# Expert rows: from a scatter into two rows per token to an accumulating scatter into one, with the surplus branch moved behind the last store

## The chip, the cores and the metric

The kernel runs on one core of one Trainium2 chip. The metric is the device time of one execution in microseconds (us). The core has five engines with a queue each: TensorE (PE, matrix products), VectorE (DVE), ScalarE (ACT), GpSimd (POOL) and SyncE (SP, which here only issues DMAs). Data moves between DRAM and the on-chip memory SBUF by DMA; an indirect DMA takes its row numbers from a table and is issued from POOL.

## The reference

The input x has 16 batches of 256 tokens with 256 values, 4096 tokens in all. Each batch has a profile number that selects an adapter, and the layer-normed output of the adapter goes through a shared two-layer network and through the two best of eight experts:

```python
z = relu(x @ Wd[profile] + bd[profile])
y = x + z @ Wu[profile] + bu[profile]
h = (y - mean(y)) * rsqrt(var(y) + 1e-5) * g[profile] + b[profile]

p = softmax(h @ gate_w + gate_b)                 # 8 experts
value, index = top_k(p, 2)
value = value / (sum(value) + 1e-9)
mlp(h, w1, b1, w2, b2) = gelu(h @ w1 + b1) @ w2 + b2     # 256 -> 1024 -> 256
moe = sum over the 2 experts of value[e] * mlp(h, ew1[e], eb1[e], ew2[e], eb2[e])
out = x + h + mlp(h, sh_w1, sh_b1, sh_w2, sh_b2) + moe
```

## The kernel before

**Numbers.** Every float32 operand of a large product is split into two float16 halves, and three of the four half products are summed. So a product `mm1` or `mm2` is a group of six matmuls.

**Order.** Nearly all instructions are entered with `plan.op(engine, duration, function, v, deps, acq, rel, after=...)`. `Plan.schedule` works out a start for each from the given durations and due times `v`, and this gives the order in which each engine's queue is written. The real waits are set by the compiler's semaphores from what each instruction reads and writes. An engine works through its queue in order.

**Stages.** `base` (SBUF, 32 tiles of 128 tokens by 256 values) holds the sum that becomes the output.

1. Adapter, layer norm, gate and routing, batch by batch. `payload` makes the split activation rows. `route` finds the two experts of each token and its slot, POOL writes the token's row numbers behind the payload (L1100), and an indirect DMA scatters the rows to their slots in DRAM, `xslot` (L1111). `table` counts slots, pads them and works out which blocks exist. Beside this, PE runs the shared network on batches 0 to 12 (`shared`), whose result is added to `base` (L1355).
2. Experts. There are 37 units: 16 static ones (two blocks of 256 tokens for each expert, weights prepared by `Prep`), 16 dynamic ones of 256 tokens, and 5 of 128 tokens, whose weights are loaded again from `scr` (`block_weights`). `block_T` loads a unit's rows transposed and its row numbers `idt`. `plan_unit` runs the first product, the activation and the split (`hh`), `plan_g2` the second product. On each of the 69 result tiles of 128 tokens, DVE scales it and adds the bias (`take`, L1261, into one of four buffers `ysb`; the profile calls that space `late`), and POOL scatters it with an indirect DMA to `yrow` in DRAM, which has two rows for each token (`scatter_y`, L1267). `apart` declares that these scatters never touch the same rows, so none waits for another.
3. During the dynamic units, ACT's queue reloads x (L1555) and POOL adds x and the shared bias to `base` (L1562, L1563). For the first six batches (`EARLY`), SP loads the rows of `yrow` written by the static units (L1523), DVE adds them with their routing weight `wts` (`sum_one`, L1534), and SP stores the batch (L1539). The weights come from `top2_weights`.
4. After the last expert unit and the first product of shared batch 13, all engines reach a branch (L1631). It is taken only where more blocks exist than the static program covers, or where an early batch has rows beyond the static units; for these inputs it is jumped over.
5. Behind it: the rest of batch 13, batches 14 and 15, the loads of `yrow` for batches 6 to 15 (five of 1 MB), the weighted sums (L1689 on ACT, L1696 on DVE, L1704 on POOL), ten stores.

Of the kernel before, what the change touches and what calls it, by code (L numbers as in the profile page):

```python
# [19 lines left out]
P = 128  # L20
# [15 lines left out]
TOP_AT = 18  # L36
EARLY = 6
# [7 lines left out]
PW = 544  # L45
NBUF = 3
# [98 lines left out]


P_V = (82.0, 121.0)
PACE = (0.0, 9.6, 24.7, 16.4)
VE2 = 8.9

TV, WV, PU2, VP = 22.0, 21.0, 10.32, 8.0
# [3 lines left out]
def adapter_moe_kernel(  # L155
# [25 lines left out]
    yrow = dp.tile([2 * NT, D], F32, tag="yrow", name="yrow")  # L181
# [50 lines left out]
    idb = [const([P, 2, 2], F16, f"idt{i}") for i in range(8)]  # L232
    idx_half = const([P, 2, 2], F16, "idh")
# [45 lines left out]
    plan.pool("id", 8)  # L279
    plan.pool("ysb", 4)  # L280
# [23 lines left out]
    def constants():  # L304
# [50 lines left out]
        )  # L355

    metaf = const([1, 2, NFULL], I32, "metaf")
    metah = const([1, NHALF], I32, "metah")
    used = const([P, 2], I32, "used")
# [355 lines left out]
    def plan_unit(  # L715
# [8 lines left out]
        for c in range(NC):  # L724
# [20 lines left out]
            if c % 4 == 3:  # L745
                def hi(act, q=q, hb=hb):
                    split_hi(hhb[plan.slot["hh", k]], h32b[plan.slot["h32", hb]], tail, q, n, act)

                def lo(q=q, hb=hb):
                    split_lo(hhb[plan.slot["hh", k]], h32b[plan.slot["h32", hb]], tail, q, n)  # L750

                h = plan.op(
                    ("DVE", "ACT") if free_hi else "ACT",
                    ((0.87, 1.1) if full else (0.5, 0.65)) if free_hi else 1.1,
                    (lambda hi=hi: hi(False), lambda hi=hi: hi(True))
                    if free_hi else (lambda hi=hi: hi(True)), vc + 1.0,
                    [ge[-1]], acq=[("hh", k)] if q == 0 else (), lat=0.05,
                )
                quads.append(
                    plan.op(  # L760
                        "DVE", 1.28 if full else 0.7, lo, vc + 2.0, [h], rel=[("h32", hb)], lat=0.05
                    )
                )
# [262 lines left out]
    def route(g):  # L1026
# [68 lines left out]
        for b in (2 * g, 2 * g + 1):  # L1095
            prev = []
            for c in range(2):
                it = plan.op(
                    "POOL", 0.2,
                    lambda b=b, c=c: POOL.iota(  # L1100
                        payb[plan.slot["pay", b]][:, :, 2 * D : PW].bitcast(I32),
                        pattern=[[2 * P, 2], [0, (PW - 2 * D) // 2]],
                        base=4 * P * b + c, channel_multiplier=2,
# [32 lines left out]
    def table(last):  # L1136
        def rt(shape, dt, name):
# [3 lines left out]
        pc2 = lambda: pt_of("count")[:, E : 2 * E]  # L1141
        cnt = plan.op(
            "PE", 0.2,
            lambda: (
                PE.matmul(pc(), ones, mc[:, NG, :], start=True, stop=True),
                PE.matmul(pc2(), ones, mc[:, EARLY // 2, :], start=True, stop=True),
            ), 0.0,
# [10 lines left out]
        over = rt([P, 1], F32, "over")  # L1158
# [5 lines left out]
        for e in range(E):  # L1164
# [12 lines left out]
            lambda: V.tensor_reduce(over, pc2(), AX.X, ALU.max),  # L1177
# [47 lines left out]
        def meta():  # L1225
# [11 lines left out]
            V.tensor_scalar(over, over, float(NSTAT * BLK), 64.0, ALU.is_gt, ALU.mult)  # L1237
            V.tensor_copy(used[:, 0:1], ends[:, 1, E - 1 : E])
            V.tensor_scalar(used[:, 1:2], over, ends[:, 1, E - 1 : E], None, ALU.add)
# [9 lines left out]
    def block_T(u, xgT, idt):  # L1249
        for t in range(u["nt"]):  # L1250
# [7 lines left out]
            SP.dma_start(idt[:, t, :], src[:, 2 * D : 2 * D + 2])  # L1258
# [5 lines left out]

    def scatter_y(ysb, idt, t):
        POOL.memset(spot, 0.0)
        ins = POOL.indirect_dma_start(  # L1267
            out=yrow[:, :],
            out_offset=bass.IndirectOffsetOnAxis(ap=idt[:, t, :].bitcast(I32), axis=0),
            in_=ysb,  # L1270
            in_offset=None,
            bounds_check=2 * NT - 1,
            oob_is_err=False,
        )
        apart("ysc", ins)
# [74 lines left out]
    def shared(b, v, only1=False):  # L1350
        def evac(t, mm, v, rel):
            dst = base[:, 2 * b + t, :]
            plan.op(
                "DVE", 0.45,
# [3 lines left out]
            )  # L1358
# [3 lines left out]
            [tc_done[b]], pE.done, [pE.tail1], free_hi=only1, only1=only1,  # L1362
            behind=g1_last[NU - 1] if only1 else None,
        )

    for b in range(NSH):
        shared(b, U0 + b * PU)
# [7 lines left out]
    plan.op(  # L1375
        "SP", 0.45, lambda: SP.dma_start(sb2_b, sb2.partition_broadcast(P)), 150.0, land=P * 1024
    )
    prep = {}
# [13 lines left out]
    sc_last, W, g1_of, vu_of = {}, {}, {}, {}  # L1392

    def expert_unit(s, vu):
# [27 lines left out]

        def evac(t, mm, v, rel):
            if nt == 1:
                rel = (*rel, ("wf", ("half", s)))
            ty = plan.op(
                "DVE", 0.45,
                lambda: take(ysbb[plan.slot["ysb", (s, t)]], py_of(t, ("e", s)), u["tail"]),
                v, [mm, *ev_deps], acq=[("ysb", (s, t))], rel=rel,
            )  # L1430

            def sc():
                scatter_y(ysbb[plan.slot["ysb", (s, t)]], idb[plan.slot["id", s]], t)

            sc_last[s] = plan.op(
                "POOL", 1.36, sc, v + 0.5, [ty], after=[sc_last.get(s, sc_last.get(s - 1))],
                rel=[("ysb", (s, t))] + ([("id", s)] if t == nt - 1 else []), land=P * 1024,
# [7 lines left out]
        g1_last[s], g1_of[s], vu_of[s] = g1[-1], g1, vu  # L1445
# [6 lines left out]
    for e in range(E):  # L1452
        if e >= 2:
# [3 lines left out]
            else:  # L1457
# [3 lines left out]
                after = [ev_last[NSTAT * (e - 3)] if e > 3 else pads[-1]]  # L1461
            prep[e] = Prep(e, v_of(NSTAT * (e - 1)) - VP, after=after, split_after=split)
# [4 lines left out]


    wts = const([P, 2, NTILE], F32, "wts")
    wlate = const([P, 2, 2 * EARLY], F32, "wlate")  # L1470

    def top2_weights(v):
        T8 = [P, NTILE, E]
        rs, den = const([P, NTILE], F32, "rs"), const([P, NTILE], F32, "den")
        rk, beyond = const([P, 2, 2 * EARLY], I32, "rk"), const([P, 2, 2 * EARLY], F32, "beyond")
        tmp, ex = [z.rearrange("p (j e) -> p j e", e=E) for z in ztb]
        o = plan.op(
            "DVE", 0.4,
            lambda: V.tensor_tensor(tmp, L, m1.unsqueeze(2).broadcast_to(T8), ALU.subtract),
            v, [*gate_of.values(), sli_of[NG - 1], *ydone.values(), ev_last[12]],  # L1480
        )
        o = plan.op("ACT", 3.0, lambda: ACT.activation(ex, tmp, AF.Exp), v, [o])
        fns = [lambda: V.tensor_reduce(rs, ex, AX.X, ALU.add), lambda: V.reciprocal(rs, rs)]
        for c in range(2):
            fns += [
                lambda c=c: V.tensor_tensor(tmp, ex, oh[:, c], ALU.mult),
                lambda c=c: V.tensor_reduce(wts[:, c, :], tmp, AX.X, ALU.add),
                lambda c=c: V.tensor_tensor(wts[:, c, :], wts[:, c, :], rs, ALU.mult),
            ]
        e2 = slice(0, 2 * EARLY)  # L1490
        fns += [
            lambda: V.tensor_tensor(den, wts[:, 0, :], wts[:, 1, :], ALU.add),
            lambda: V.tensor_scalar(den, den, 1e-9, None, ALU.add),
            lambda: V.reciprocal(den, den),
            lambda: V.tensor_tensor(
                wts, wts, den.unsqueeze(1).broadcast_to([P, 2, NTILE]), ALU.mult
            ),
            lambda: V.tensor_scalar(rk, sli[:, :, e2], EBLK * P - 1, None, ALU.bitwise_and),
            lambda: V.tensor_scalar(beyond, rk, float(NSTAT * BLK), None, ALU.is_ge),
            lambda: V.tensor_tensor(wlate, wts[:, :, e2], beyond, ALU.mult),  # L1500
            lambda: V.tensor_tensor(wts[:, :, e2], wts[:, :, e2], wlate, ALU.subtract),
        ]
        return tiny(fns, v, [o], dur=0.22, first=0.4)

    wts_op = top2_weights(0.0)
    for b in range(EARLY):
        plan.op(
            "SP", 0.5,
            lambda b=b: SP.dma_start(
                yrow[2 * b * S : 2 * (b + 1) * S, :].rearrange("(p k) d -> p k d", p=P),  # L1510
                padrow[:, 0 : 2 * D].bitcast(F32).unsqueeze(1).broadcast_to([P, 4, D]),
            ), 60.0 + 12 * b, after=[ln_done[2 * b + 4]], land=99,
        )
# [7 lines left out]

    def y_load(yl, t0, nt):
        SP.dma_start(  # L1523
            yl.rearrange("p j c d -> p j (c d)"),
            yrow[2 * P * t0 : 2 * P * (t0 + nt), :].rearrange("(j p c) d -> p j (c d)", p=P, c=2),
        )
        return yl

    def y_view(flat, nt):
        return flat.bitcast(F32).rearrange("p (j c d) -> p j c d", c=2, d=D)[:, 0:nt]  # L1530

    def sum_one(b, yl, t, c, w):
        j = 2 * b + t
        V.scalar_tensor_tensor(  # L1534
            base[:, j, :], yl[:, t, c, :], w[:, c, j : j + 1], base[:, j, :], ALU.mult, ALU.add
        )

    def store(b):
        SP.dma_start(  # L1539
# [5 lines left out]
    early_buf = [y_view(flat[:, o * 1024 : (o + 2) * 1024], 2) for o in (4, 6)]  # L1545
    plan.pool("xr", 2)
    plan.pool("ey", 2)
    wf_free = [prep[E - 1].tail, *prep[E - 1].done]
    for b in range(NB):
        s = TOP_AT + 1 + b  # L1550
        xr = xlnT[:, 2 + b % 2].rearrange("p l k s -> p (l k s)").bitcast(F32)
        xr = xr.rearrange("p (t d) -> p t d", t=2)
        o = plan.op(
            "ACT", 0.45,
            lambda b=b, xr=xr: ACT.dma_start(  # L1555
                xr, x[b * S : (b + 1) * S, :].rearrange("(t p) d -> p t d", p=P)
# [219 lines left out]
```

## Time and profile before

| | |
|---|---|
| median of 3 runs | 642.57 us (641.12 to 643.31) |
| profiled execution | 643.85 us |
| its span, first to last instruction | 642.1 us |
| PE / DVE / ACT / POOL busy | 605.6 / 405.8 / 404.3 / 234.2 us |
| expert scatters | 69, first issued at 233.8 us, last at 601.7 us |
| PE, last matmul before the branch ends | 600.9 us |
| PE, first matmul behind the branch | 604.26 us |
| last matmul / last store issued | 638.3 / 638.9 us |
| DRAM read / written | 96.46 MB / 44.42 MB |

"Busy" is the time in which an engine executes. The landing of a DMA is the time from its issue until its data is in place and its semaphore is set; for an indirect DMA the busy time on POOL is only the making of its descriptors. The DMA share is the mean busy share of the sixteen DMA engines.

### The profile page before, as it was taken

How to read it: one execution, taken by the hardware profiler on the slowest of the kernel's cores; microseconds unless marked ns; L12 is line 12 of the kernel's file. 1: busy time of each engine (PE TensorE's matmuls, PEld its weight loads, DVE VectorE, ACT ScalarE, POOL GpSimd, SP SyncE). 2: the span in 40 equal slices, each digit the busy share in tenths (PEclk: the TensorE clock that was granted, in tenths of full speed). 3: DMA queues.
4: the chain of work that ended last, by engine and by line, in shares of the span. 5: the costliest groups of instructions: out<-in, count | busy, mean ns of one | idle time of the engine just before them, and what ended most of it. 6: DMA issues, size and time to landing. Idle time of an engine off the chain costs nothing. (4 is left out here: it accounts for less than half of the span.)

```text
span 642.1 us, 15142 instructions
## 1 busy us (share of the span) xinstructions
PE 605.6 (94%) x5542; PEld 522.8 (81%) x5542; DVE 405.8 (63%) x969; ACT 404.3 (63%) x632; POOL 234.2 (36%) x370
## 2 busy tenths in 40 slices
PE   5599999999999999999999999999988998999795
PEld 3368887888988888888888888998967977888684
DVE  5688889899873643775586664455446545545287
ACT  1378576796876867988878755554554535555372
POOL 1003566185387012222221321252325483643143
PEclk7779999999999999999999999999999999999798
DMA  7885558847422276789975698559967699770292
GB/s 262 274 271 168 181 190 309 311 165 264 139 93 105 51 233 140 269 191 273 305 225 154 201 297 267 149 150 300 325 158 257 166 331 258 248 179 19 66 350 98
DMA packets 95783, 134.70 MB, mean 210 GB/s; under 512 B 53691, under 2 KB 73173, under 8 KB 87766
## 3 DMA queue, kind: packets, MB, share of 16 engines
q1 hardware_dynamic: 83778, 108.89, 56.6%
q0 software_dynamic: 6768, 18.43, 8.1%
q10 hardware_dynamic: 5156, 6.35, 3.3%
q8 instruction: 45, 0.74, 0.5%
q14 instruction: 36, 0.29, 0.2%
HBM read 96.46 MB, written 44.42 MB: 219 GB/s over the span
## 5 line engine op out<-in xcount | busy, mean ns | idle before, releaser
L704 PEld LDWEIGHTS <-hh 128*128 128x128 f16 x2424 | 235.1, 98 | 38.4 <-DVE hh L689 9.8
L675 ACT ACTIVATE h<-bank,tst 128x256 f32<-128x256 f32 x256 | 136.0, 560 | 127.8 <-PE bank L668 86.8
L704 PE MATMUL bank<-wst,hh 128*128 128x256 f16 x1536 | 205.8, 273 | 3.3 <-DVE hh L689 3.3
L668 PE MATMUL bank<-late,wst 128*128 128x256 f16 x1536 | 200.4, 273 | 5.0 <-ACT h L675 4.3
L1267 POOL DMA_INDIRECT yrow<-late,idt x69 | 77.6, 1125 | 256.7 <-DVE late L1261 202.6
L668 PEld LDWEIGHTS <-wst 128*128 128x128 f16 x1536 | 150.1, 98 | 23.3 <-issue 4.8
L668 PE MATMUL bank<-xlnT,wsh 128*128 128x256 f16 x768 | 106.6, 279 | 3.4 <-ACTq L1631 3.4
L704 PE MATMUL bank<-wsh,hh 128*128 128x256 f16 x768 | 104.7, 277 | 3.4 <-DVE hh L689 3.4
L675 ACT ACTIVATE h<-bank,tsh 128x256 f32<-128x256 f32 x128 | 70.1, 560 | 58.7 <-PE bank L668 55.1
L689 DVE SCALAR_TENSOR_TENSOR hh<-h,tst,hh 128x1024 f16<-128x1024 f32 x64 | 89.4, 1396 | 27.5 <-ACT hh L683 26.0
L668 PEld LDWEIGHTS <-wsh 128*128 128x128 f16 x768 | 75.5, 100 | 15.5 <-issue 3.8
L1111 POOL DMA_INDIRECT xslot<-late,sli x64 | 70.4, 1101 | 38.5 <-issue 22.4
L1261 DVE SCALAR_TENSOR_TENSOR late<-bank,tst 128x256 f32<-128x256 f32 x64 | 30.5, 483 | 65.0 <-PE bank L704 64.8
L685 DVE TENSOR_SCALAR hh<-h,tst 128x1024 f16<-128x1024 f32 x27 | 21.3, 787 | 46.3 <-ACT h L675 46.3
L689 DVE SCALAR_TENSOR_TENSOR hh<-h,tsh,hh 128x1024 f16<-128x1024 f32 x32 | 42.0, 1311 | 13.4 <-ACT hh L683 13.1
L683 ACT ACTIVATE hh<-h,tst 128x1024 f16<-128x1024 f32 x37 | 42.5, 1148 | 1.1
L683 ACT ACTIVATE hh<-h,tsh 128x1024 f16<-128x1024 f32 x29 | 33.3, 1147 | 0.8
L1100 POOL IOTA late<- 128x32 int32 x32 | 4.8, 161 | 73.4 <-PE bank L977 37.8
L623 DVE SCALAR_TENSOR_TENSOR wst<-wf,prep,wst 128x1024 f16<-128x1024 f32 x20 | 25.3, 1279 | 0.7 <-ACT wst L617 0.7
L842 PE MATMUL bank<-xlnT,wst 128*128 128x256 f32 x64 | 20.6, 453 | 4.7 <-DMA wst<-in_adp_dram 4.7
L1563 POOL TENSOR_TENSOR base<-base,sb_b 128x512 f32<-128x512 f32 x16 | 24.2, 1515 | 1.3
L1562 POOL TENSOR_TENSOR base<-base,xlnT 128x512 f32<-128x512 f32 x16 | 20.6, 1285 | 8.2 <-DMA xlnT<-in_x_dram 8.0
(234 smaller groups left out, 582.2 us busy)
## 6 DMA issues: line engine op xcount, KB each, us to landing
wst<-scr SPq DMA_DIRECT2D x32, 1024.0 KB
scr<-wst SPq DMA_DIRECT2D x16, 1024.0 KB
wf<-scr SPq DMA_DIRECT2D x10, 1024.0 KB
wf<-in_ew_dram SPq DMA_DIRECT2D x5, 1028.0 KB
wf<-in_ew_dram SPq DMA_DIRECT2D x5, 1024.0 KB
wst<-in_adp_dram SPq DMA_DIRECT2D x16, 256.5 KB
xlnT<-in_xT_dram SPq DMA_DIRECT2D x16, 256.0 KB
base<-in_x_dram SPq DMA_DIRECT2D x16, 256.0 KB
```

Source lines behind the costliest of these rows:

```text
L623: V.scalar_tensor_tensor(self.w[:, a + 2048 : b + 2048], self.wf[h][:, f], sc[:, 2 * h : 2 * h + 1], self.w[:, a:b], ALU.mult, ALU.subtract,)
L668: mm = PE.matmul(pa[:, 0:n_tok], w1[:, wl, c, k, :], xin[:, xl, k, 0:n_tok], start=i == 0, stop=i == len(seq) - 1,)
L675: ACT.activation(h32[:, c % 4, 0:n_tok], pa[:, 0:n_tok], AF.Gelu_apprx_tanh, bias=tail[:, c : c + 1], scale=tail[:, 8:9],)
L683: ACT.activation(hi, h4, AF.Copy, scale=tail[:, 9:10])
L685: V.tensor_scalar(hi, h4, tail[:, 9:10], None, ALU.mult)
L689: V.scalar_tensor_tensor(hh[:, 1, c, 0:n_tok], h32[:, :, 0:n_tok], tail[:, 9:10], hh[:, 0, c, 0:n_tok], ALU.mult, ALU.subtract,)
L704: PE.matmul(py, hh[:, hl, k, t * P : (t + 1) * P], w2[:, wl, k, :], start=q == 0 and i == 0, stop=q == 3 and i == len(seq) - 1,)
L842: PE.matmul(pt_of(("z", b))[:, 0:S], wa()[:, k * P : (k + 1) * P], xf32(b)[:, k, :], start=k == 0, stop=k == KC - 1,)
L1111: ins = POOL.indirect_dma_start(out=xslot[:, :], out_offset=bass.IndirectOffsetOnAxis(ap=sli[:, c, j : j + 1], axis=0), in_=payb[plan.slot ...
L1261: V.scalar_tensor_tensor(ysb, py, tail[:, 10:11], tail[:, 11 : 11 + D], ALU.mult, ALU.add)
L1267: ins = POOL.indirect_dma_start(out=yrow[:, :], out_offset=bass.IndirectOffsetOnAxis(ap=idt[:, t, :].bitcast(I32), axis=0), in_=ysb, in_of ...
L1563: POOL.tensor_tensor(bb, bb, sb2_b.unsqueeze(1).broadcast_to([P, 2, D]), ALU.add)
```

## The change

- `yrow` (two rows a token) becomes `yacc` (one row a token, 128 more for padding). Four DMAs from DRAM to DRAM fill it with x (`y_init`) during the first stage. The reload of x and its addition on POOL go.
- Each payload row carries two numbers: where its routing weight lies in a table `wtab` in DRAM, and its token's row.
- `top2_weights` runs before the experts and is written to `wtab`. For each result tile POOL fetches 128 weights with an indirect DMA (`row_weights`), and DVE multiplies the tile by them.
- The scatter adds to the rows of `yacc` (`compute_op=ALU.add`). It is no longer declared free of overlap with the other scatters.
- All of the loads of the sums (now 16 of 256 KB), the additions and the stores come after the last scatter. The early sums and stores go.
- The branch stands behind the last store, and the two plans become one. Some due times and modelled durations are set anew.

```diff
-P_V = (82.0, 121.0)
-PACE = (0.0, 9.6, 24.7, 16.4)
-VE2 = 8.9
-TV, WV, PU2, VP = 22.0, 21.0, 10.32, 8.0
+P_V = (91.71, 94.73)
+PACE = (0.0, 9.24, 25.25, 16.52)
+VE2 = 7.08
+TV, WV, PU2, VP = 29.65, 21.1, 10.37, -5.15
+SC_LAT = 3.0
+W_AT, X_AT, X_STEP = 178.0, 100.0, 15.0
...
+    def row_weights(wq, idt, t):
+        POOL.memset(spot, 0.0)
+        POOL.indirect_dma_start(
+            out=wq[:, t : t + 1],
+            out_offset=None,
+            in_=wtab[:, :],
+            in_offset=bass.IndirectOffsetOnAxis(ap=idt[:, t, 0:2].bitcast(I32), axis=0),
+        )
+
     def scatter_y(ysb, idt, t):
         POOL.memset(spot, 0.0)
-        ins = POOL.indirect_dma_start(
-            out=yrow[:, :],
-            out_offset=bass.IndirectOffsetOnAxis(ap=idt[:, t, :].bitcast(I32), axis=0),
+        POOL.indirect_dma_start(
+            out=yacc[:, :],
+            out_offset=bass.IndirectOffsetOnAxis(ap=idt[:, t, 2:4].bitcast(I32), axis=0),
             in_=ysb,
             in_offset=None,
-            bounds_check=2 * NT - 1,
-            oob_is_err=False,
-        )
-        apart("ysc", ins)
+            compute_op=ALU.add,
+        )
...
+    y_init = [
+        plan.op(
+            "SP", 0.5,
+            lambda i=i: SP.dma_start(yacc[i * TG : (i + 1) * TG, :], x[i * TG : (i + 1) * TG, :]),
+            X_AT + X_STEP * i, after=[X_GATE[i]], land=TG * 1024,
+        )
+        for i in range(NT // TG)
+    ]
...
+        for t in range(nt):
+            wq_of[s, t] = plan.op(
+                "POOL", 1.36,
+                lambda t=t: row_weights(wqb[plan.slot["wq", s]], idb[plan.slot["id", s]], t),
+                vu + 3.0 + t, [BT[s], wts_op, wts_pad],
...
+            scaled_y = plan.op(
+                "DVE", 0.3,
+                lambda: V.tensor_scalar(
+                    ysb(), ysb(), wqb[plan.slot["wq", s]][:, t : t + 1], None, ALU.mult
+                ), v, [ty, wq_of[s, t]], rel=[("wq", s)] if t == nt - 1 else (),
...
             sc_last[s] = plan.op(
-                "POOL", 1.36, sc, v + 0.5, [ty], after=[sc_last.get(s, sc_last.get(s - 1))],
-                rel=[("ysb", (s, t))] + ([("id", s)] if t == nt - 1 else []), land=P * 1024,
+                "POOL", 1.36, lambda: scatter_y(ysb(), idb[plan.slot["id", s]], t), v + 0.5,
+                [scaled_y, *y_init, sc_last.get(s, sc_last.get(s - 1))],
+                rel=[("ysb", (s, t))] + ([("id", s)] if t == nt - 1 else []), lat=SC_LAT,
             )
...
+    g1 = g1_last[NU - 1]
+    for b in range(NSH, NB):
+        g1 = shared(b, v_end + (b - NSH) * PU2, behind=g1)[-1]
...
     for b in range(NB):
...
+        ld_y = plan.op(
+            "SP", 0.5, lambda b=b: y_load(y_buf[b], 2 * b, 2), v_end + b,
+            [sc_last[NU - 1], *ring_free], land=P * 2048,
+        )
         o = plan.op(
...
+            "DVE", 0.69, lambda b=b: sum_y(b), v_end + 4.0 + 1.5 * b,
+            [ld_y] + (last_evac[b] if b < NSH else []),
+        )
+        plan.op("SP", 0.5, lambda b=b: store(b), v_end + 9.0 + 1.5 * b, [o, *last_evac[b]])
...
-        any_left = nc.values_load(used[0:1, 1:2], min_val=0, max_val=most + 64)
-        with tc.If(any_left > 2 * NFULL + SURE):
-            count = nc.values_load(used[0:1, 0:1], min_val=0, max_val=most)
-            with tc.If(count > 2 * NFULL + SURE):
+        count = nc.values_load(used[0:1, 0:1], min_val=0, max_val=most)
+        with tc.If(count > 2 * NFULL + SURE):
```

## The prediction

> **What bounds the kernel now.** I read the busy times first, then busy time by stretches, then the waits of PE, and last the line of the scatter, since the change works on that.
>
> ```profile
> PE 605.6 (94%) x5542; PEld 522.8 (81%) x5542; DVE 405.8 (63%) x969; ACT 404.3 (63%) x632; POOL 234.2 (36%) x370
> ```
>
> PE is the bound: 605.6 of 642.1 us. The stretches say where the rest is (columns: busy us and instructions of PE, its weight loads, DVE, ACT, POOL, then granted clock, DMA share, GB/s):
>
> ```profile
> 230.00:602.00 372.00, 359.92 (x3398) 321.09 (x3396) 202.31 (x294) 231.97 (x374) 129.42 (x169) 1.00 0.76 220
> 600.00:604.30 4.30, 0.94 (x10) 0.70 (x8) 1.77 (x2) 1.71 (x2) 1.14 (x3) 0.86 0.23 74
> 604.30:610.20 5.90, 5.90 (x30) 4.24 (x30) 0.00 (x0) 1.13 (x2) 0.00 (x0) 0.53 0.48 139
> 631.00:638.40 7.40, 4.07 (x24) 2.76 (x22) 7.26 (x13) 0.00 (x0) 1.80 (x2) 0.77 0.32 108
> ```
>
> The reader is to see 12 us of PE idle in the expert stage, 3.4 at the branch, then a slow clock (0.53), and 3.3 near the end. The waits of PE and of ACT between 430 and 592 us name the first:
>
> ```profile
> PE bank L668 <- ACT h L675: 6.3, 4, 2.5
> PE bank L704 <- DVE hh L689: 3.9, 6, 1.2
> ...
> ACT h L675 <- DMA out_dram<-base: 6.2, 1, 6.2
> ACT h L675 <- POOL base L1562: 5.3, 2, 3.0
> ...
> ACT h L675 <- DMA xlnT<-in_x_dram: 2.1, 1, 2.1
> ```
>
> PE waits for activations that stand in ACT's queue behind reloads of x, whose buffers were not free. Now the scatters:
>
> ```profile
> L1267 POOL DMA_INDIRECT yrow<-late,idt x69: 966/983/1894, 233.8 to 601.7; - x69
> ...
> DMA to landing us min/median/max: 2.4/4.6/8.9
> ```
>
> Making the descriptors takes 1 us, landing 2.4 to 8.9. Nobody waits for a landing here, so nothing of it is in the 642 us.
>
> **What the change removes.** (1) The x reloads, their additions (16 x 1.285 us of POOL, L1562) and the early sums (24 x 0.547 us of DVE, L1534) leave the dynamic units. Of the 10.2 us of PE waits shown I count 7 as gone; the shorter ones need a DVE in time, and it stays loaded. (2) At the branch PE loses 3.4 us, and then five groups of six matmuls take 1.28 us each where later ones take 0.655: 3.1 us more. Both go. (3) The late weighting (L1689, L1696, L1704) goes; one addition of 128x512 per batch replaces it (nearest row L873, 0.687 us; 16 x 0.687 = 11 us of DVE under PE's last 26 us).
>
> **What it adds beside other work.** 69 weight fetches on POOL at 1.125 + 0.132 us (rows L1267, L1266) are 87 us; with the 20.6 taken away POOL is busy 129 + 66 = 195 of 372 us: hidden, and a fetch is due a whole unit before its use. If that cover went, DVE would stand before its multiplication for a landing. 69 multiplications on DVE: between 0.2 us (a quarter of L685's 0.787 for 1024 columns) and 0.48 (L1261), I take 0.3, 21 us less the 13 of the early sums; DVE goes from 202 to 210 of 372: hidden by PE. Row numbers (16 more iotas of 0.16 us) and the weights' arithmetic, moved from 367 us to about 180, fall before the experts, where POOL's longest stretch is 25.8 of 40 us: 0 to 2 us, I take 0. The fill of `yacc` is four DMAs of 1 MB on SP's queue among the layer stage's loads; it replaces six zero fills of 512 KB there (L1509), where the DMA share is 0.65 to 0.78: 0 to 3 us, I take 0. New due times: -3 to 3 us, I take 0.
>
> **What it adds on a chain.** The scatters are no longer declared apart, and an addition reads before it writes, so each must wait until the one before it has landed. This wait stands on POOL's queue. Behind it stand the fetches for later units and the next scatter; a late scatter keeps its `ysb` buffer, `take` on DVE then waits for one of the four, the splits stand behind `take`, and PE behind the splits. So 69 landings in a row become a second possible bound. Their room: from 233.8 us to the last `take`, 601.4, less the 7 us above: 360 / 68 = 5.3 us each.
>
> What is a landing in this stage? Asked one by one, 26 of the 69 have one recorded; their mean is 5.0 us (sum 130.3). They go with the load. The rows below are stretches from issue to landing, of 6.8, 7.3, 2.5 and 2.4 us:
>
> ```profile
> 267.50:274.30 6.80, 6.80 (x65) 6.08 (x64) 3.02 (x6) 6.29 (x10) 1.09 (x2) 1.00 0.99 410
> 309.70:317.00 7.30, 7.30 (x69) 6.54 (x68) 3.52 (x6) 5.01 (x8) 1.09 (x2) 1.00 1.03 402
> 494.20:496.60 2.40, 1.29 (x18) 1.11 (x16) 2.37 (x3) 0.00 (x0) 2.30 (x3) 1.00 0.31 109
> 503.50:506.00 2.50, 2.50 (x25) 2.24 (x24) 0.48 (x1) 0.00 (x0) 2.40 (x3) 1.00 0.33 109
> ```
>
> Full DMA engines make it 7, idle ones 2.4: a plain landing is 2.4 fixed and 2.6 on average behind the weight loads, which stay.
>
> Here row and rule part. The Trainium skill ("DMA: Bandwidth & Descriptors", section "Anatomy of one DMA — SWDGE (gpsimd) path") gives about 2.0 us plus bytes over 436 GB/s for a DMA issued from POOL: 2.3 us for 128 KB, as the emptiest rows agree. By it the chain takes 69 x about 3 = 207 us and never binds; the estimate would be the 634 us of the first rival. The rows under load say 5.0, and I go by them.
>
> One cycle of the chain: 5.0 landing; 0.25 to hand over (memset 0.132, two queue instructions of 0.03 and 0.04, semaphore); and the addition. No row shows an accumulating DMA. From below it costs 0 (it does all that the plain one does and reads more, so no gain). From above, a rule: an adding transfer has two source reads on one ring ("Collectives: The Full Stack", section "The bandwidth ceiling: the fold count and why AG ≠ RS ≠ AR"), half the rate; no run here shows it. If the loaded part doubles and one fixed read of 0.3 is added: 2.9. I take 0.7, near the lower end, since the idle row shows most of a landing to be latency, and one DRAM read is a part of it. The same bytes over a stage stretched by a tenth load the engines less: 0.2 off the loaded 2.6. Cycle: 5.0 + 0.25 + 0.7 - 0.2 = 5.75 us.
>
> Chain: 235 (first issue, a unit start 1 us later) + 69 x 5.75 = 632 us, 30 us behind the present end of the experts. A unit with two scatters (11.5 us) is then 1.2 us slower than PE's 10.3 us of it; once the four buffers are full, PE stands still by that much in each unit. Its clock should hold: the wait of 2.5 us above left it at 1.00.
>
> **The end.** All sums are loaded after the last landing: 4.2 MB in, 4.2 MB out. The stretch from 610 to 631 us ran at 290 GB/s, its best slice on the page at 350: at 320, 26 us. Now 3.2 us pass from the last store's issue (638.9) to the end; the branch comes on top, since SP must jump and the engines meet: 0 (hidden under the landing) to 4 (PE's jump took 4.01 us at 599.4), I take 1.5. Sum: 31 us. PE's remaining 26 us of batches 13 to 15 lie beneath it.
>
> Span: 632 + 31 = 663. The profiled execution took 1.75 more than its span and stands 1.3 above the median: **664 us**.
>
> **Rivals.**
> - *The chain keeps pace* (other side, faster). The addition is nearly free and the load lighter, cycle 5.2 or less. The experts end at 594, the last pair lands near 602, the end takes 31: 633, or **634** on the median's scale. For it: 7 us of idle and 6.5 at the branch really go, and the idle landings of 2.4. Against it: landings of 6.8, 7.0 and 7.3 between 267 and 317 us, and it decides at a cycle of (642 - 31 - 235) / 69 = 5.45, which plain landings with their hand-over (5.25) all but use up.
> - *The adding transfer queues twice* behind the loads. Cycle 5.0 + 0.25 + 2.9, less 1.0 for thinner load, 7.1: 235 + 490 + 31 = **757**. For it: loaded landings three times the idle ones, so it is waiting in queues that counts. Against it: row descriptors of 1 KB may wait once for both reads. Here PE would idle over 3 us at a time, and the 0.53 clock after the branch shows what follows.
> - *The waits do not appear*, and scatters overlap as now: this gives the 634 too. Against it: the declaration is struck out in the diff.
>
> **How the numbers follow.** Chain binds near 664: 0.56. Queues twice: 0.12. Keeps pace, by either way: 0.27. Between, within 0.3% of 642.6 (what a measurement can tell, about 2 us): 0.05. So faster 0.27, same 0.05, slower 0.68. The range begins at 633, leaving out some 0.08 below, and ends at 720, a cycle of 6.6, leaving out 0.12. The likeliest case's own range is 648 to 700 (cycles of 5.5 to 6.3).
>
> **What would show it.** Right: POOL before a scatter waits for the DMA into `yacc`; scatters of a unit stand 5 to 8 us apart instead of 1.3 to 2.6; `take` waits for such a landing; the last scatter is issued near 626. The branch's step: no gap with a slow clock behind it near 600. The end's step: first `yacc` load to last store about 27 us. Wrong: landings of adding scatters at 2.4 to 4 us under full load, or scatters of a unit issued without that wait; then the time is the 634.

## The result, and the profile after

| | before | after |
|---|---|---|
| median of 4 runs, us | 642.6 (641.12 to 643.31) | 716.5 (715.25 to 721.99) |
| ratio to before | 1 | 1.117 (95%: 1.1108 to 1.1232) |
| profiled execution / its span, us | 643.85 / 642.1 | 715.62 / 713.8 |
| first scatter issued, us | 233.8 | 244.9 |
| from the first to the last scatter, us | 367.9 | 436.1 |
| from the last scatter to the end, us | 40.4 | 32.7 |

The change costs 74 us, where 21 were forecast. Of the 71.7 us between the spans, 11.1 arise before the first scatter, 68.2 between the scatters, and 7.7 come back behind them.

The busy times of the page of after:

```profile
PE 625.2 (88%) x5541; PEld 530.0 (74%) x5541; DVE 404.5 (57%) x998; ACT 403.4 (57%) x617; POOL 335.0 (47%) x507
```

PE is busy 20 us longer than before, yet its share fell from 94% to 88%: it is idle for 89 us of the span, and its matmuls take longer. One row for the expert stage and three 40 us stretches of it (columns as in the prediction: busy us of PE, its weight loads, DVE, ACT, POOL, granted clock, DMA share, GB/s) say both:

```profile
320.00:640.00 320.00, 272.76 (x2424) 235.09 (x2422) 141.11 (x210) 158.36 (x257) 171.31 (x207) 0.94 0.69 169
...
360.00:400.00 40.00, 34.04 (x282) 28.82 (x283) 22.55 (x40) 23.81 (x35) 22.98 (x27) 0.90 0.53 131
400.00:440.00 40.00, 31.98 (x265) 27.04 (x264) 9.93 (x16) 17.49 (x27) 13.56 (x18) 0.93 0.74 189
...
640.00:680.00 40.00, 37.68 (x365) 33.61 (x364) 18.13 (x27) 20.38 (x36) 19.30 (x24) 1.00 0.26 31
```

Before, PE was busy 359.92 of 372 us here, at a clock of 1.00. Now it stands still for 47 of 320 us, no other engine is near its limit, and the DMA engines carry less than before. So nothing is full, and the stage is bound by a latency. The waits of the whole span name it (columns: total us, times, longest):

```profile
DVE late L1269 <- DMA yacc<-late,idt: 139.6, 35, 7.2
POOL yacc L1284 <- DVE late L1269: 128.2, 40, 9.8
...
PE bank L712 <- DVE hh L697: 48.7, 17, 5.5
...
POOL yacc L1284 <- DMA yacc<-late,idt: 17.1, 7, 4.5
```

PE waits for a split (L697; 41.1 of the 48.7 us lie in the stage), the split stands on DVE behind `take` (L1269), and `take` waits until a scatter into `yacc` has landed and set its buffer free. The second line seems to say that the scatter waits for `take`, in a circle. The timelines of POOL and of DVE around 406 us show what it is (start, duration; idle before in brackets):

```profile
397.89 1.68 POOL L1284 DMA_INDIRECT yacc<-late,idt  x1 [0.30 <-DVE late L1269]
...
406.90 1.66 POOL L1284 DMA_INDIRECT yacc<-late,idt  x1 [5.46 <-DVE late L1269]
...
414.31 1.64 POOL L1284 DMA_INDIRECT yacc<-late,idt  x1 [4.35 <-DVE late L1269]
```

```profile
406.23 0.48 DVE L1269 SCALAR_TENSOR_TENSOR late<-bank,tst 128x256 f32<-128x256 f32 x1 [5.75 <-DMA yacc<-late,idt]
406.75 0.35 DVE L1513 TENSOR_SCALAR late<-late,wq 128x256 f32<-128x256 f32 x1
...
413.63 0.48 DVE L1269 SCALAR_TENSOR_TENSOR late<-bank,tst 128x256 f32<-128x256 f32 x1 [6.53 <-DMA yacc<-late,idt]
```

The scatter at 406.90 begins before the weighting of that tile (L1513, 406.75 to 407.10) has ended, so it carries an older tile. The round after it shows what let both go: the scatter of 406.90 lands 6.6 us later, at 413.5; `take` starts at 413.63 and the next scatter at 414.31. It is one event, and the profile puts the scatter's wait down to the instruction that ended just ahead of it. Both rows mean the chain.

The cycle itself is plainest near the end, where no weights are loaded any more (POOL's timeline; then, for the line of the scatter from 666.5 to 673 us, POOL's semaphore waits with min/median/max in ns and first and last start, and the landings):

```profile
663.14 1.55 POOL L1284 DMA_INDIRECT yacc<-late,idt  x1 [2.86 <-DMA yacc<-late,idt]
...
667.67 1.55 POOL L1284 DMA_INDIRECT yacc<-late,idt  x1 [2.87 <-DMA yacc<-late,idt]
...
672.21 1.55 POOL L1284 DMA_INDIRECT yacc<-late,idt  x1 [2.70 <-issue]
```

```profile
L1284 POOLq EVENT_SEMAPHORE  x2: 17/2022/4026, 667.0 to 667.5; - x2
...
DMA to landing us min/median/max: 3.7/3.8/3.8
```

The scatter of 667.67 lands 3.8 us later, at 671.47. POOL's wait, begun at 667.5 and 4.03 us long, ends at once, at 671.5. But the next scatter starts only at 672.21. A cycle is the landing plus 0.74 us, 4.54 in all; the next two are 4.42 and 4.43. Over the whole stage (`yacc` in after):

```profile
L1284 POOL DMA_INDIRECT yacc<-late,idt x69: 1549/1645/2912, 244.9 to 681.1; - x69
...
DMA to landing us min/median/max: 3.6/4.6/12.3
```

Making the descriptors takes 1.65 us where the plain scatter took 0.98; the emptiest landing is 3.6 where it was 2.4. The trace has 39 of the 69 landings, with a mean of 5.65 us; the 68 steps from scatter to scatter have a mean of 436.1 / 68 = 6.41. Behind 36 of the 38 recorded landings that have a successor, the next scatter starts 0.72 to 0.79 us after the landing, behind the other two 1.33 and 2.06. So wherever the trace can tell, the chain is closed but for two places, from the first scatter to the last.

The branch's gap in the middle is gone. Behind the experts PE stops once more, for 4.54 us before 689.71, since a split stands on DVE behind the first of the sums, and the clock is 0.63 in the 4 us after that; experiment 1 has no such stop and the same way to the end (32.5 us), so this cost next to nothing. At the end SP loads 16 batches of sums from 684.95, the last store is issued at 706.6, and the program ends at 713.8.

### The profile page after: what moved, and what is told of

The parts are those of the page before. It is cut to its first block, busy times and chain, and to the rows that moved or that the text cites. A ratio compares the mean times of both kernels' runs of the same rounds, so it can differ in the third digit from the quotient of the medians.

```text
span 713.8 us, 15285 instructions
## 1 busy us (share of the span) xinstructions
PE 625.2 (88%) x5541; PEld 530.0 (74%) x5541; DVE 404.5 (57%) x998; ACT 403.4 (57%) x617; POOL 335.0 (47%) x507
## 3 DMA queue, kind: packets, MB, share of 16 engines
q0 software_dynamic: 15600, 19.12, 14.6%
## 5 line engine op out<-in xcount | busy, mean ns | idle before, releaser
L712 PE MATMUL bank<-wst,hh 128*128 128x256 f16 x1536 | 218.4, 281 | 41.1 <-DVE hh L697 41.1
L683 ACT ACTIVATE h<-bank,tst 128x256 f32<-128x256 f32 x256 | 139.8, 561 | 170.4 <-PE bank L676 118.3
L676 PE MATMUL bank<-late,wst 128*128 128x256 f16 x1536 | 208.8, 278 | 9.2 <-ACT h L683 9.2
L1284 POOL DMA_INDIRECT yacc<-late,idt x69 | 120.6, 1748 | 202.0 <-DVE late L1269 128.2
L1127 POOL DMA_INDIRECT xslot<-late,sli x64 | 75.1, 1173 | 116.5 <-DVE rs_t L932 46.4
L1269 DVE SCALAR_TENSOR_TENSOR late<-bank,tst 128x256 f32<-128x256 f32 x64 | 30.8, 483 | 168.2 <-DMA yacc<-late,idt 123.7
L697 DVE SCALAR_TENSOR_TENSOR hh<-h,tst,hh 128x1024 f16<-128x1024 f32 x64 | 81.6, 1280 | 17.5 <-ACT hh L691 16.7
L1275 POOL DMA_INDIRECT wq<-wtab,idt x69 | 78.1, 1132 | 25.2 <-DMA idt<-xslot 15.0
L697 DVE SCALAR_TENSOR_TENSOR hh<-h,tsh,hh 128x1024 f16<-128x1024 f32 x32 | 40.9, 1280 | 11.2 <-ACT hh L691 11.1
L1274 POOL MEMSET spot<- 128x1 f32 x69 | 33.9, 491 | 0.0
L1513 DVE TENSOR_SCALAR late<-late,wq 128x256 f32<-128x256 f32 x69 | 29.5, 429 | 1.9
L683 ACT ACTIVATE h<-bank,late 128x128 f32<-128x128 f32 x40 | 15.6, 451 | 18.4 <-DVE hh L697 14.2
```

Source lines behind the costliest of these rows:

```text
L676: mm = PE.matmul(pa[:, 0:n_tok], w1[:, wl, c, k, :], xin[:, xl, k, 0:n_tok], start=i == 0, stop=i == len(seq) - 1,)
L683: ACT.activation(h32[:, c % 4, 0:n_tok], pa[:, 0:n_tok], AF.Gelu_apprx_tanh, bias=tail[:, c : c + 1], scale=tail[:, 8:9],)
L697: V.scalar_tensor_tensor(hh[:, 1, c, 0:n_tok], h32[:, :, 0:n_tok], tail[:, 9:10], hh[:, 0, c, 0:n_tok], ALU.mult, ALU.subtract,)
L712: PE.matmul(py, hh[:, hl, k, t * P : (t + 1) * P], w2[:, wl, k, :], start=q == 0 and i == 0, stop=q == 3 and i == len(seq) - 1,)
L1127: ins = POOL.indirect_dma_start(out=xslot[:, :], out_offset=bass.IndirectOffsetOnAxis(ap=sli[:, c, j : j + 1], axis=0), in_=payb[plan.slot ...
L1269: V.scalar_tensor_tensor(ysb, py, tail[:, 10:11], tail[:, 11 : 11 + D], ALU.mult, ALU.add)
```

## The experiments

**Theory A**: the time is the chain of 69 landings, made longer than PE's own pace by the addition. **Theory B**: POOL's queue, with its 69 weight fetches and longer descriptors, stretches the cycle. Beside them stood the start, which came 10 us late, and the branch. The first four kernels ran together; there before took 643.47 us.

**1. The wait without the addition.** The sums are then left out: of x and the two results for a token only what was written last remains.

```diff
             in_=ysb,
             in_offset=None,
-            compute_op=ALU.add,
         )
```

> The changed kernel with the scatter writing its rows instead of adding them; the wait for the scatter before stays. This leaves out the addition. Theory A (a chain of landings, one cycle = landing + 0.75 us, and the addition makes a landing 1.3 us longer, by the emptiest landings 3.7 against 2.4): the cycle falls from 6.4 to about 5.1, just under the 5.3 that PE needs, so the time falls to 645 to 660. Theory B (the chain is not the landings but POOL's queue: weight fetches, memsets and descriptor making between the scatters): the queue holds the same instructions, so the time stays at 705 to 716.

Measured: 641.66 us, ratio 0.9969 (0.9945 to 0.9993). With a serial chain of 69 plain scatters the whole takes as long as before, a little less than I had expected. POOL's timeline (from start to start is a cycle), the landings, and the busy row of the stage:

```profile
584.10 0.98 POOL L1284 DMA_INDIRECT yacc<-late,idt  x1 [0.81 <-DVE hh L697]
...
587.29 0.98 POOL L1284 DMA_INDIRECT yacc<-late,idt  x1 [0.81 <-DMA yacc<-late,idt]
...
590.44 0.97 POOL L1284 DMA_INDIRECT yacc<-late,idt  x1 [0.78 <-issue]
```

```profile
DMA to landing us min/median/max: 2.4/3.3/7.8
```

```profile
230.00:615.00 385.00, 379.96 (x3569) 339.44 (x3567) 222.81 (x333) 245.10 (x390) 187.76 (x285) 0.99 0.70 195
```

Scatters 3.2 us apart with landings of 2.4: the hand-over is 0.75 to 0.8 without the addition too, so it belongs to the wait. The 25 recorded landings have a mean of 4.46 us. With 0.75 that is 5.2 a cycle, the pace at which PE delivers tiles where no chain holds it (354.7 / 68 = 5.22 in experiment 2). So this chain stands at the edge, and it is not free: behind 20 of the 25 landings the next scatter still follows after 0.74 to 0.79 us, PE works 380 of 385 us, and the stage takes 365 us where experiments 2 and 3 take 355. What takes the chain well over that edge is the addition: 75 us between this kernel and after, for one argument.

**2. The addition without the chain.** Two accumulators take scatters in turn, and each waits for the one before last. 16 more loads and additions at the end put the two together; the second one is filled with zeros.

```diff
-                "POOL", 1.36, lambda: scatter_y(ysb(), idb[plan.slot["id", s]], t), v + 0.5,
-                [scaled_y, *y_init, sc_last.get(s, sc_last.get(s - 1))],
+                "POOL", 1.36,
+                lambda: scatter_y(ysb(), idb[plan.slot["id", s]], t, (yacc, yac2)[n % 2]), v + 0.5,
+                [scaled_y, *y_init, *sc_all[-2:-1]], after=sc_all[-1:],
```

> The changed kernel with two accumulators: scatters go to them in turn, so each waits for the one before the last; one is filled with x, the other with zeros, and both are loaded and added at the end (4.2 MB more). Theory A: each chain has 10.6 us of room for a cycle of 6.4, so PE sets the pace again, the last scatter is issued near 610, and the end grows by about 14 us: 650 to 660. Theory B: POOL's queue is no shorter, the last scatter stays near 680 and the time is 720 to 730.

Measured: 648.69 us, ratio 1.0082 (1.0054 to 1.011). The busy row of its expert stage:

```profile
240.00:605.00 365.00, 365.00 (x3467) 328.66 (x3465) 210.65 (x323) 236.76 (x377) 228.29 (x279) 1.00 0.84 202
```

PE has no gap at all and its clock is 1.00. The same adding scatters land no sooner here (ten recorded landings of 3.8 to 8.8 us, 7.2 in the median), but each now has the time of two tiles, 2 x 5.22 us, and holds nobody up. What it gains in the stage it spends at its ends: 13 us of later start, and 44.2 us from the last scatter to the end instead of after's 32.7, for loads of 8.4 MB instead of 4.2.

**3. Neither.** Plain scatters of the weighted tiles into two rows a token, declared apart as before; two rows are loaded for the sum. x is left out of the output.

```diff
-        POOL.indirect_dma_start(
-            out=yacc[:, :],
+        ins = POOL.indirect_dma_start(
+            out=yrow[:, :],
...
-            compute_op=ALU.add,
+        apart("ysc", ins)
```

> The changed kernel with plain scatters of the weighted rows into two rows per token, declared free of overlap as in the kernel before; no fill with x, so x is left out of the sum, and twice the bytes are loaded at the end. Theory A: no chain at all, the last scatter near 605 to 610, 645 to 655 in all. Theory B: 700 or more.

Measured: 643.24 us, ratio 0.999 (0.9966 to 1.0013). Its expert stage:

```profile
240.00:605.00 365.00, 365.00 (x3467) 328.68 (x3466) 211.71 (x335) 238.84 (x379) 183.57 (x277) 1.00 0.68 196
```

Beside experiment 2 this row prices the addition in throughput: the DMA share falls from 0.84 to 0.68 at nearly the same GB/s, and POOL from 228 to 184 us. PE doesn't feel either. So weighting early and fetching the weights cost PE nothing within the stage; what the stage gains is spent at its two ends (table below).

**4. No weight fetch.** The tile is multiplied by 0.5; the routing weights are left out.

```diff
-            wq_of[s, t] = plan.op(
-                "POOL", 1.36,
-                lambda t=t: row_weights(wqb[plan.slot["wq", s]], idb[plan.slot["id", s]], t),
...
-                    ysb(), ysb(), wqb[plan.slot["wq", s]][:, t : t + 1], None, ALU.mult
+                    ysb(), ysb(), half[:, 0:1], None, ALU.mult
```

> The changed kernel without the 69 weight fetches; every result row is multiplied by 0.5 instead. This leaves out the routing weights. Theory A: the adding chain stays; only what the fetches take of the DMA rings and of POOL's turn between two scatters goes, 0.2 to 0.4 us in a cycle: 685 to 703. Theory B: 87 us of POOL's queue go, and the time falls to 640 to 660.

Measured: 705.61 us in two runs, ratio 1.0967 (1.088 to 1.1054). The chain is still there, 427.4 / 68 = 6.29 us a cycle, with recorded landings of 5.60 in the mean. Theory B falls as the cause: the fetches are not it, and the longer descriptors do not fill POOL's queue, which is busy 228 of 365 us with them in experiment 2. Within the chain, though, the making of the descriptors stands inside each landing; what that comes to is worked out below. And the fetches are not quite free either: 0.13 us a cycle, 8.7 us in all, which the prediction had put at nothing. Its interval and that of after just miss each other.

The stages of the kernels so far, and of one that follows, from the trace of each (us):

| | first scatter | first to last | last to end | span |
|---|---|---|---|---|
| before | 233.8 | 367.9 | 40.4 | 642.1 |
| after | 244.9 | 436.1 | 32.7 | 713.8 |
| 1 wait, no addition | 243.0 | 365.0 | 32.5 | 640.5 |
| 2 two accumulators | 246.4 | 354.7 | 44.2 | 645.3 |
| 3 plain, two rows | 243.6 | 354.8 | 43.0 | 641.4 |
| 4 no weight fetch | 244.2 | 427.4 | 32.8 | 704.5 |
| 8 apart in a unit, old due times | 238.9 | 357.6 | 32.7 | 629.2 |

All that hold the new due times start their scatters 9 to 13 us later than before; those that the chain does not hold (2, 3 and 8) run through the stage 10 to 13 us faster than before. Experiments 1 to 3 came out 1 to 3 us below what theory A had led me to expect, and experiment 4 came out 3 us above it.

**5. The old due times, in the changed kernel.** This and the next three ran on another chip, where before takes 665.5 us, so only ratios are compared with the others.

```diff
-P_V = (91.71, 94.73)
-PACE = (0.0, 9.24, 25.25, 16.52)
-VE2 = 7.08
-TV, WV, PU2, VP = 29.65, 21.1, 10.37, -5.15
+P_V = (82.0, 121.0)
+PACE = (0.0, 9.6, 24.7, 16.4)
+VE2 = 8.9
+TV, WV, PU2, VP = 22.0, 21.0, 10.32, 8.0
```

> The changed kernel with the due times of the kernel before (P_V, PACE, VE2, TV, WV, PU2, VP). Its first scatter is issued at 244.9 us, 11 later than before. If the new due times make that, it comes back by 5 to 11 us with the chain behind it unchanged: 706 to 711. If the moved arithmetic of the weights or the fill with x makes it, the time stays at 714 to 719.

Measured: ratio 1.1053 (1.0923 to 1.1183), not told apart from the 1.117 of after. But the first expert product starts at 239.92 us, and in the kernels with the new times on that chip at 251.80 and 256.18. With before's times and before's scatters (next item) it starts at 239.25. So on this chip the late start comes from the new due times and not from the work that was moved there; which of the numbers does it was not singled out. The trace of experiment 8, from another chip, agrees only in part: with the old times its first scatter is still 5 us later than that of before.

**6. No branch, in before and in after.** The whole block under the If and the jump are left out of both.

```diff
-        any_left = nc.values_load(used[0:1, 1:2], min_val=0, max_val=most + 64)
-        with tc.If(any_left > 2 * NFULL + SURE):
...
```

> The kernel before without its branch. If the gap of 3.4 us and the slow clock of 3.1 us behind it are what the branch costs: 635 to 638. If the sums and stores behind it set the end anyway: 640 to 643.

> The changed kernel without the surplus branch, which is never taken with these inputs. If SP's jump behind the last store costs what the trace suggests (4.5 us from its compare to its next instruction, part of it under the landing of the store), 4 us go: 712 to 713. If it is hidden under the landing: 716 to 717.

Measured: before without it has a ratio of 0.9922 (0.9876 to 0.9967), 5.2 us of 665.5 (2 to 8 by the interval): the branch did cost about what its gap and slow matmuls showed. After without it has 1.1099 (1.1014 to 1.1184), beside 1.117 (1.1108 to 1.1232) with it: this doesn't settle what the branch costs at the end. The trace says that it can't be much. From the last store's issue to the end after takes 7.2 us and this kernel still 6.5, since twelve stores stand in SP's queue until then (its timeline):

```profile
726.20 8.12 SPq L1583 DMA_DIRECT2D out_dram<-base  x12
```

**7. Only the two scatters of a unit apart.** A unit has one expert, and an expert gets a token once, so the rows of its two tiles differ, but for padding rows, which are dropped here by a bound on the row number. Each scatter then waits only for those of the unit before.

```diff
-    def scatter_y(ysb, idt, t):
+    def scatter_y(ysb, idt, t, unit=None):
...
             compute_op=ALU.add,
+            bounds_check=NT - 1,
+            oob_is_err=False,
         )
+        if unit is not None:
+            apart(f"y{unit}", ins)
...
-                [scaled_y, *y_init, sc_last.get(s, sc_last.get(s - 1))],
+                [scaled_y, *y_init, *sc_all.get(s - 1, [])], after=[sc_last.get(s)],
```

> The changed kernel with the two adding scatters of a unit declared free of overlap with each other (one expert, so their tokens differ), and padding rows dropped by a bound instead of written; only scatters of different units wait for each other. Theory A: a cycle is then one pair of overlapping landings, about 8 us in a unit of 10.3, so PE sets the pace, the last scatter is issued near 608 and the end of 29 us follows: 637 to 643. Theory B: 700 or more. A third way: the two landings do not overlap, since one DMA ring serves both, and a pair takes 10 to 11 us: 650 to 670.

Measured: ratio 0.9983 (0.9945 to 1.0021). One wait fewer in each unit takes the whole loss away. The scatters are 357.75 / 68 = 5.26 us apart, PE's pace; its expert stage, in which PE idles 2 us:

```profile
240.00:600.00 360.00, 357.92 (x3378) 321.38 (x3376) 211.89 (x322) 235.89 (x372) 214.80 (x266) 1.00 0.85 202
```

**8. The same with the old due times.** The edits of 5 and 7 together. This, the next one and a second run of after ran on a third occasion, where before took 642.26 us.

> The two adding scatters of a unit declared free of overlap with each other, padding rows dropped, and the due times of the kernel before. In the runs so far the first expert product came 11 us or more earlier with the old due times, and with pairs apart PE sets the pace: 0.978 to 0.986 of the kernel before, faster than both kernels. If the pairs' chain is what sets the pace after all, the earlier start is lost again: 0.995 to 1.002.

Measured: **631.5 us (631.0 to 632.42), ratio 0.9837 (0.9802 to 0.9872)**, faster than both kernels. Its expert stage:

```profile
220.00:590.00 370.00, 366.25 (x3469) 328.53 (x3467) 217.05 (x331) 242.30 (x383) 236.57 (x288) 1.00 0.84 199
```

PE idles 4 us where it idled 12 in before; the adding scatters, the fetches and the late sums are all in it. By the table it starts 5.1 us later than before, makes up 10.3 among the experts and 7.7 behind them.

> The changed kernel itself, beside the others on this chip: 1.11 to 1.12 of the kernel before.

After itself, beside it: 720.49 us, ratio 1.1224 (1.1185 to 1.1263).

**9. Before, with x reloaded from POOL's queue instead of ACT's.**

```diff
-            "ACT", 0.45,
-            lambda b=b, xr=xr: ACT.dma_start(
+            "POOL", 1.3,
+            lambda b=b, xr=xr: POOL.dma_start(
```

> The kernel before with the 16 reloads of x issued from POOL's queue instead of ACT's. If the activations that stood behind those reloads cost PE its 6.3 us in the dynamic units, the ratio to the kernel before is 0.989 to 0.993. If PE waits there for something else (weights, DVE), 0.997 to 1.003.

Measured: 642.81 us, ratio 1.0008 (0.9989 to 1.0027). PE's waits for activations between 430 and 592 us fell from 6.3 to 0.4 us and its busy time there rose by 3.4 to 154.4 of 162, but nothing reached the end: the experts started 2 us later, and the last scatter was issued at 602.9 instead of 601.7. A wait of 2.5 us for a unit's rows came in their place. The queue was one cause of the idle time, and taking it away alone brings nothing.

Not tried: adding scatters with no waits at all, since two experts of one token add to the same row. Not separated: how much of the longer landing is the making of the descriptors and how much the transfer, since both come with the addition.

## Why the prediction was right in kind and wrong in size

**The bound, and who waits for whom: right.** The chain of landings took PE's place. POOL's wait, `take` behind the buffers and PE behind the splits stand in the profile as foretold, and the loss goes where waits are taken out (experiments 2 and 7) and where each link is made shorter (experiment 1).

**The failed step: the cycle of 5.75 us.** It is 6.38 over the 69 (684.95 less 244.92), 43 of the missing 51 us; the later start makes 10 more, and the end gives 2 back. Its terms:

| term | predicted | measured | from |
|---|---|---|---|
| plain landing, thinner load taken off | 5.0 - 0.2 | 4.46 | experiment 1, 25 records |
| addition | 0.7 | 1.2 | after's mean 5.65 less 4.46; idle 3.7 less 2.4 = 1.3 |
| hand-over | 0.25 | 0.75 | 671.47 to 672.21 in after; the same in experiment 1 |
| sum | 5.75 | 6.4 | |

Two terms were too small by half a microsecond each, and one gave 0.3 back. The hand-over I had added up from instructions that POOL's queue showed for a wait on DVE, and for such a wait it was right: in before `take` ends at 244.04 and its scatter starts at 244.33. For a wait on a DMA the semaphore is as prompt, and the time passes between the end of the wait and the start of the next scatter. For the addition, the prediction had no term for the longer making of the descriptors, which a landing, counted from the issue, contains. Of the landings with idle engines above, POOL's instruction takes 1.55 of 3.7 us with the addition and 0.98 of 2.4 without. So about 0.6 of the 1.3 us stand there and 0.7 behind it, if the one follows the other, which no run here shows. Ends had been named for the addition, 0 and 2.9; taking 0.7, near the lower one, was the wrong choice, since even an idle landing grew by half of itself. The means of 25 and 39 of 69 landings are samples: a second run of after, with a cycle of 6.38, has a mean of 5.23 over the 34 that its trace has. So the split between the first two terms is less firm than their sum.

**The start at 235 us: wrong, 10 us.** The new due times were put at nothing between -3 and 3. Experiment 5 shows that they delay the first expert product by some 12 us on its chip; by the table, 6 of the 11 us go with the old times here. In experiments 7 and 8, where no chain hides it, they are worth about 1.5% of the time by the two ratios (0.9837 / 0.9983), which come from two chips and by their intervals leave 0.7 to 2.2%.

**The clock should hold: wrong.** One stall of 2.5 us in before had left it at 1.00. PE's waits between 230 and 660 us in after, 16 of up to 5.7 us and 50.3 us in all, go with a clock of 0.90 to 0.96 in every stretch of 40 us from 320 to 640. The length of a stall does not decide it alone. PE's timeline behind two of them and the rows of the stretches that follow:

```profile
399.34 1.04 PE L712 MATMUL bank<-wst,hh 128*128 128x256 f16 x4 [2.42 <-DVE hh L697]
...
431.89 0.61 PE L712 MATMUL bank<-wst,hh 128*128 128x256 f16 x4 [3.81 <-DVE hh L697]
```

```profile
399.30:403.30 4.00, 3.96 (x22) 2.97 (x23) 1.18 (x1) 1.13 (x2) 1.94 (x4) 0.59 1.01 403
...
432.00:440.00 8.00, 8.00 (x75) 7.14 (x75) 2.35 (x4) 4.60 (x8) 2.01 (x4) 1.00 0.38 51
```

Behind 2.42 us of idle the clock is at 0.59, behind 3.81 at 1.00. So the stall of 2.5 us in before was no proof that such a stall is harmless: it had got through, and one just as long in after did not. The Trainium skill ("TensorE: Matmul & The Clock Gate", section "HAM oscillation — how this bites in real kernels") warns of gaps over about 3.4 us; this trace does not bear that limit out, since the gap of 2.42 was followed by the slow clock and the one of 3.81 was not. What decides it was not found. The prediction had counted 1.2 us of standstill in each unit of two tiles and not asked in what pieces it would come. I count no term for the clock in the sum, since PE has time to spare while the chain binds; that was not tested by itself.

**The weight fetches at nothing: not quite.** Experiment 4 finds about 9 us with the chain closed. They were hidden for PE; for the chain, which runs over the same queue, they probably were not; behind 39 of experiment 4's 42 recorded landings the next scatter starts after 0.72 us, where after has mostly 0.76 to 0.79, which makes some 3 of the 9. The place of the rest within a cycle was not found.

**The end at 31 us: right**, 28.9 from the first load of sums to the end. The branch there was to cost 0 to 4; by experiment 6's trace the stores cover nearly all of it. Its gain of 6.5 at the old place measured 5.2. The forecast of it was a little high already: the five slow groups of matmuls take 6.0 us together (from 604.26 to the start of the sixth at 610.26), 2.7 more than five later ones and not 3.1. **The 7 us from the x reloads and early sums**: the stage is shorter by more than that wherever the chain is open (10 to 13 us in the table), but experiment 9 shows that taking the reloads out of ACT's queue alone does not bring it; what does was not singled out.

**The rivals.** "Keeps pace" decided at 5.45 a cycle, and the plain chain of experiment 1, at 365.0 / 68 = 5.37, is the case it described; the addition passed the point. "Queues twice" took 2.9 us for the addition, where 1.2 was measured; its cycle of 7.1 was 0.7 too long, about as far off as the forecast was short. The Trainium skill's rule for a transfer issued from POOL, weighed in the prediction ("DMA: Bandwidth & Descriptors", section "Anatomy of one DMA — SWDGE (gpsimd) path"), gave 2.3 us: the emptiest landing of experiment 1 is 2.4, but the mean under load is 4.46, so the rows were the right guide.

## What to carry to other kernels

When transfers that overlapped must follow one another, latency times their number becomes a bound, though no engine is full: add up one whole cycle, with the time from landing to the next start and the operation's own price, and compare it with the pace at which the bound engine delivers. Where the sum comes within some 10% of that pace, as here (5.75 against 5.3), the answer hangs on terms of half a microsecond, so look for a way not to need every wait: here the two scatters of one unit could never meet, and saying so turned 1.12 into 1.00, and into 0.98 with the old due times. Take the price of a hand-over from a wait of the same kind: here 0.28 us behind an engine and 0.75 behind a DMA. Price new due times as a change of their own: these cost some 1.5%, and beside the chain it could not be told.

## What the runs showed of the hardware

- An adding indirect DMA of 128 rows of 1 KB takes 1.65 us of POOL for its descriptors, where the plain one takes 0.98 to 1.0, and lands in 3.6 us at best, where the plain one does in 2.4. The software queue carries 15600 packets in after and 8976 in experiment 1 (96 more for each scatter), and their share of the sixteen DMA engines rises from 9.0% of 640.5 us to 14.6% of 713.8, 0.68 us of all sixteen for each scatter.
- From a landing until the next indirect DMA starts on POOL, 0.75 us pass, in which the trace of after shows no work on POOL, though the wait itself ends within 0.07 of the landing. In before, 43 of the 69 scatters start 0.28 us after the end of `take`, on which they wait.
- The granted clock was 0.90 to 0.96 in 40 us stretches of after with 2 to 8 us of PE idle. Behind a stall of 2.42 us it was 0.59 for the next 4 us, behind one of 3.81 us it stayed at 1.00.
- PE's jump over the branch took 5.9 us at the end of after, longer than the 4.0 in before; there it lies beside the draining stores.
